# Order of the table work inside a look-up slot: low part and first count behind the look-ups, second count ahead of its pieces, table last

## The chip, the cores and the metric

The kernel runs on one core of a Trainium2 chip. The metric is the device time of one execution in microseconds. Before the change the median of three runs is 6,190.36 us (6,180.27 to 7,300.34).

## The reference, cut to what matters

Four graph layers over 16 graphs of 1,024 nodes with 128 features, each followed by a residual and a layer norm. The part that the change touches computes layer 1, the others run beside it or after it.

```python
# layer 0: masked attention over adj
# layer 1: for every node the maximum over its neighbours
p = jnp.einsum('bnd,do->bno', x, W1 - W2)
q = jnp.einsum('bnd,do->bno', x, W2)
pre = p[:, :, None, :] + q[:, None, :, :] + b
h = jax.nn.relu(pre) * adj[..., None]
out = jnp.max(h, axis=2)
# layer 2: sum over neighbours and a two-layer perceptron
# layer 3: a row-by-row thinning ("dilation") of adj that depends on the
#          rows before, then three graph convolutions with batch norms
```

## The kernel before, in words

The maximum over neighbours is done by tables. The 1,024 possible neighbours of a graph are cut into groups of six; for each group a table holds the maximum of q over each of its 64 subsets, and a node needs the entry of the subset that its row of the adjacency selects. Two groups (12 neighbours) make one **slot** s; a graph has NP = 86 slots, 16 graphs have 1,376. The look-up is a matmul with a one-hot matrix: 64 rows for one group, 64 for the other. Everything else that layers 0 to 2 and the dilation need is cut into **pieces** that are spread among the slots.

The names in `slot(s, last)`, which writes the order of the four engines out by hand (a manual schedule; a queue runs in the order in which the code is met):

- `look_up(s, i, pg)` (L839 to L845): four matmuls for half i (512 nodes) of slot s, the high and the low part of the table times the one-hot `hot`, into `pg`, a tile of two PSUM banks (tag "wide", two buffers). Both halves are looked up at the start of a slot. The VectorE line L911 takes the maximum of `pg` into `best`, once for each half.
- `count(s, h)` (L807 to L815): for half h of slot s one matmul counts on how many of the six neighbours each node's row agrees with each subset (`pm`, L814), and ScalarE turns the count into the one-hot `hot` (L815). `hot` has three buffers; the count runs two slots ahead of its look-up.
- `table(s)` (L817 to L830), every second slot: two transposes on TensorE bring the subset table of two slots from nodes by subsets into `pt` (L826); ScalarE copies it, rounded, to `high` (L829).
- `low_part(s)` (L832 to L836), every second slot, one slot later: a matmul subtracts `high` from `pt` in place (L834), and ScalarE copies the remainder to `low` (L836).
- `pm` and `pt` are tiles of one tag, "subset", with two buffers of a bank each.
- `advance(engines)` (L786 to L805) issues pieces: each stream (scores, attend, rest, tables_of) yields the engine and the cost of its next piece, and a piece is issued when the engine has room in this half slot, when its delay since the piece before has passed and when one of two "shared" PSUM banks is free, all by a virtual time `now` that counts slots. It is called for TensorE first, then for ScalarE, VectorE and GpSimd. `dilate_on()` does the same for the dilation, which has due times in slots.

A slot is worked in two halves, h = 0 and 1. In each half the order is: (half 0: both look-ups), pieces of TensorE, pieces of the others, a dilation piece, (half 0 of odd slots: low part), count of slot s + 2 for this half, (half 1 of even slots: table), `best` for this half. A piece of TensorE that VectorE evacuates is mostly evacuated in the next half slot; one that ScalarE evacuates, in the same one.

Of the kernel before, what the change touches and what calls it, by code (L numbers as in the profile page):

```python
# [74 lines left out]
def tile_graph_layers(ctx: ExitStack, tc, a, out):  # L75
# [166 lines left out]
    def layers_012():  # L242
# [133 lines left out]
        def attend(b):  # L376
            for t in range(T):
                yield ask("PE", 0.01, after=("e", b, t))
                if t == 0:
                    y = w4.tile([P, T, D], F32, name="y0", tag="xT")  # L380
                e, total = exps.pop((b, t))
                eT = w4.tile([P, T, P], F32, name="eT")
                for h in range(2):
                    yield ask("PE", 0.44, take=True, same=(h == 0))
                    p = shared("pe")
                    for c in range(4):
                        nc.tensor.transpose(p[:, c * P:(c + 1) * P],
                                            e[:, (4 * h + c) * P:(4 * h + c + 1) * P], ident)
                    yield ask("A", 0.59, give=True, same=True)
                    nc.scalar.copy(eT[:, 4 * h:4 * h + 4, :].rearrange("p c i -> p (c i)"), p)  # L390
                happened["back", b, t] = now
                for h in range(4):
                    yield ask("PE", 0.45, take=(h == 0), same=(h > 0))
                    if h == 0:
                        pav = shared("pav")[:, :D]
                    for c in range(2 * h, 2 * h + 2):
                        nc.tensor.matmul(pav, eT[:, c, :], values[b][:, c, :], start=(c == 0), stop=(c == T - 1))  # L397
                yield ask("V", 0.4, give=True)
                share = small.tile([P, 1], F32, name="share")
                nc.vector.reciprocal(share, total)  # L400
                nc.vector.scalar_tensor_tensor(y[:, t, :], pav, share, X[b][:, t, :], op0=ALU.mult, op1=ALU.add)
            yield from norm(X[b], y)
            happened["X1", b] = now
# [66 lines left out]
        def tables_of(b):  # L470

            if b:
                yield ask("V", 0, urgent=True, after=("tables", b - 1))
            for g0 in range(0, NP, TG):
                n_g = 2 * min(TG, NP - g0)
                yield ask("V", 0.01, same=True, urgent=True, after=("q", b))
                made.append((b, g0))
                yield ask("V", 0.1, same=True, urgent=True, after=("used", *made[-3]) if len(made) > 2 else None)
                qg = qs[b].rearrange("o (g s) -> o g s", s=GS)
                subs[b, g0] = w2.tile([P, TG, P], F32, name="sub", bufs=2)  # L480
                sub = subs[b, g0].rearrange("o t (a s) -> o (t a) s", a=2)
                nc.vector.memset(sub[:, :n_g, 0:1], LOWEST)
                for k in range(GS):
                    n = 1 << k
                    yield ask("V", 0.06 + n * n_g / 960, same=(n < 8), urgent=True)
                    nc.vector.tensor_max(sub[:, :n_g, n:2 * n], sub[:, :n_g, 0:n],  # L486
                                         qg[:, 2 * g0:2 * g0 + n_g, k:k + 1].to_broadcast([P, n_g, n]))
                happened["sub", b, g0] = now
            happened["tables", b] = now
# [255 lines left out]
        def load_x(b):  # L745
            X[b] = apool.tile([P, T, D], F32, name="X", bufs=3)
            nc.sync.dma_start(out=X[b], in_=x[b].rearrange("(t p) d -> p t d", p=P))
# [29 lines left out]
        def start(stream, first=False):  # L777
            pending[stream] = [next(stream, None), -9]
            streams.insert(0 if first else len(streams), stream)
# [27 lines left out]
        def count(s, h):  # L807

            b, g = divmod(s, NP)
            c, r = divmod(g, PC)  # L810
            if h == 0:
                hots[s] = w2.tile([P, N], F32R, name="hot", bufs=3)
            pm = psum.tile([P, 512], F32, tag="subset", name="pm", bufs=2)
            nc.tensor.matmul(pm, lit[:, r, :], AT[b * (T + 1) + c][:, halves[h]], start=True, stop=True)  # L814
            nc.scalar.activation(hots[s][:, halves[h]], pm, AF.Relu, bias=one_less)  # L815

        def table(s):  # L817

            b, g = divmod(s, NP)
            g0 = g - g % TG  # L820
            assert ("sub", b, g0) in happened, (s, [(x.__name__, pending[x]) for x in streams], room)
            pt = psum.tile([P, 512], F32, tag="subset", name="pt", bufs=2)[:, :2 * P]
            if g + 2 - g0 == min(TG, NP - g0):
                happened["used", b, g0] = now
            for k in range(2):
                nc.tensor.matmul(pt[:, k * P:(k + 1) * P], subs[b, g0][:, g - g0 + k, :], ident, is_transpose=True,  # L826
                                 start=(k == 0), stop=(k == 1))
            high = w2.tile([P, 2 * P], F32R, name="high", bufs=2)
            nc.scalar.copy(high, pt)  # L829
            tables[s] = pt, high  # L830

        def low_part(s):  # L832
            pt, high = tables[s]
            nc.tensor.matmul(pt, less, high, start=False, stop=True, skip_group_check=True)  # L834
            low = w2.tile([P, 2 * P], F32R, name="low", bufs=2)
            nc.scalar.copy(low, pt)  # L836
            tables[s] = high, low

        def look_up(s, h, pg):  # L839

            at = s % 2
            for k, part in enumerate(tables[s - at]):
                for a in range(2):
                    rows = slice(64 * a, 64 * a + 64)
                    nc.tensor.matmul(pg[:, a], part[rows, at * P:(at + 1) * P], hots[s][rows, halves[h]],  # L845
                                     start=(k == 0), stop=(k == 1))
# [16 lines left out]
        def slot(s, last):  # L863

            nonlocal now
            now = s
            b, g = divmod(s, NP)
            if s >= 0 and g == 0:
                bests[b] = bests[b - 1] if b else w4.tile([P, 2, N], F32, name="best")
                if b + 1 < B:  # L870
                    start(tables_of(b + 1), True)
                    load_x(b + 1)
                    start(attend(b + 1))
                    start(scores(b + 1))
            if s >= 0 and g % PC == 0:
                load_columns(b * (T + 1) + g // PC + 2)
            for h in range(2):
                now = s + 0.5 * h
                for e in ROOM:
                    room[e] = min(room[e] + ROOM[e] / 2, ROOM[e] / (2 if e in ("PE", "V") else 1))  # L880
                if s >= 0 and h == 0:
                    pgs = [psum.tile([P, 2, 512], F32, tag="wide", name="pg", bufs=2) for _ in range(2)]
                    for i in range(2):
                        look_up(s, i, pgs[i])
                early = s >= 0 and due < now
                if early:
                    dilate_on()
                advance(("PE",))
                advance(("A", "V", "Pool"))
                if s >= 0 and not early:  # L890
                    dilate_on()
                if h == 0 and s % 2 and s + 1 < last:
                    low_part(s + 1)
                if s + 2 < last:
                    count(s + 2, h)
                    if h and s % 2 == 0:
                        table(s + 2)
                if s >= 0:
                    own, pg = bests[b][:, :, halves[h]], pgs[h]
                    if g == 0:  # L900
                        if b:
                            if h:
                                merge(b - 1, h)
                            total(b - 1, h)
                        nc.vector.tensor_copy(own, pg)
                        if b and h:
                            start(rest(b - 1))
                    else:
                        if g == NP - 1 and h:
                            merge(b, 0)  # L910
                        nc.vector.tensor_max(own, own, pg)  # L911
            if s >= 0:
                hots.pop(s)
# [19 lines left out]
        with tc.manual_schedule(engines={mybir.EngineType.PE, mybir.EngineType.Activation, mybir.EngineType.DVE,  # L933
                                         mybir.EngineType.Pool}):
            for s in range(-2, B * NP):
                slot(s, B * NP)
# [10 lines left out]
            last = rest(B - 1)  # L947
# [426 lines left out]
```

## Time and profile before

| what | us |
|---|---|
| median of the runs shown | 6,190.36 |
| profiled execution, its time | 6,205.61 |
| its span on the core | 6,203.9 |
| TensorE busy | 5,426.3 (87%) |
| VectorE busy | 4,853.2 (78%) |
| ScalarE busy | 3,935.6 (63%) |
| GpSimd busy | 3,619.0 (58%) |
| mean granted TensorE clock | 0.965 |

The largest groups of instructions, by line:

| line, engine | what | count | busy us | mean ns | idle before it, us |
|---|---|---|---|---|---|
| L911 VectorE | best<-best,pg | 2,720 | 3,240.7 | 1,214 | 494.4 |
| L815 ScalarE | hot<-pm | 2,752 | 1,856.6 | 690 | 602.4 |
| L845 TensorE | pg<-hot,high | 5,504 | 1,325.7 | 477 | 254.8 |
| L845 TensorE | pg<-hot,low | 5,504 | 1,119.3 | 401 | 0.0 |
| L814 TensorE | pm<-AT,lit | 2,752 | 1,043.0 | 394 | 91.0 |
| L826 TensorE | pt<-ident,sub | 1,376 | 295.6 | 297 | 219.3 |
| L834 TensorE | pt<-high,less | 688 | 281.7 | 409 | 13.3 |
| L836 ScalarE | low<-pt | 688 | 256.4 | 373 | 504.8 |
| L829 ScalarE | high<-pt | 688 | 256.4 | 373 | 1.3 |

"Idle before it" is the time that the engine stood still just before such an instruction; the profile also says which instruction on which engine ended the wait. Matmul ends are modelled by the profiler. In rows of the list of waits the three numbers are the total in us, how often, and the longest. Weight loads (PEld) have rows of their own. In the timeline a row is the start, the duration, the engine, the line, what is written from what, how many instructions are merged in it, and in brackets the idle time before it.

### The profile page before, as it was taken

The numbers are of one execution on the slowest core, as the hardware profiler recorded it, in microseconds if no ns is written. First come the engines' busy times: TensorE is split into PE (matmuls) and PEld (weight loads), VectorE is DVE, ScalarE is ACT, GpSimd is POOL, SyncE is SP. The second block draws the span as 40 slices with busy tenths as digits, with TensorE's granted clock in tenths as the row PEclk, the third lists the DMA queues.
The fourth block names the chain that finished last, engine by engine and source line by source line (L and its number), as shares of the span: only waits on it lengthen the run. The fifth ranks groups of instructions, "written<-read, shape, count | busy, mean of one in ns | idle before, by whom it ended". The sixth has DMA issues, their size and how long they took to land.

```text
span 6203.9 us, 93371 instructions
## 1 busy us (share of the span) xinstructions
PE 5426.3 (87%) x30132; PEld 3090.5 (50%) x30250; DVE 4853.2 (78%) x7484; ACT 3935.6 (63%) x7362; POOL 3619.0 (58%) x11879
## 2 busy tenths in 40 slices
PE   5888888889898988888889898889888878999998
PEld 4545454545454545454545454545454435555654
DVE  2888888888888888888888888888888875555455
ACT  3666666666676666676667666666666554344865
POOL 2676666676666766667676767676667651110114
PEclk8999999999999999999999999999999989999999
DMA  5121213131212221222121212121121014554645
GB/s 41 12 34 23 40 23 40 23 41 24 39 23 36 28 40 24 37 30 37 27 41 25 37 27 39 24 39 25 32 31 29 15 43 124 160 142 129 218 163 191
DMA packets 496976, 334.29 MB, mean 54 GB/s; under 512 B 303338, under 2 KB 448228, under 8 KB 492388
## 3 DMA queue, kind: packets, MB, share of 16 engines
q1 hardware_dynamic: 405504, 260.29, 14.3%
q0 software_dynamic: 89008, 67.42, 12.6%
q8 instruction: 238, 3.90, 0.3%
q14 instruction: 254, 2.08, 0.1%
q10 hardware_dynamic: 1972, 0.59, 0.1%
HBM read 362.38 MB, written 133.96 MB: 80 GB/s over the span
## 4 chain that ended last, share of the span: by engine, by line
PE 29%; DVE 12%; ACT 5%; issue 3%; POOL 2%; DMA 1%; SPq 0%; DVEq 0%; ACTq 0%; POOLq 0%
PE pg L845 6%; DVE best L911 6%; PE pagg L1074 5%; PE pm L814 2%; PE po L1104 2%; ACT hot L815 2%; PE pav L397 1%; PE po L1098 1%; PE pa L439 1%; DVE sub L486 1%; PE pt L826 1%; PE pdeg L1029 1%; DVE near L1017 1%; PE pp L300 1%; PE prank L599 1%
## 5 line engine op out<-in xcount | busy, mean ns | idle before, releaser
L911 DVE TENSOR_TENSOR best<-best,pg 128x1024 f32<-128x1024 f32 x2720 | 3240.7, 1214 | 494.4 <-PE pg L845 485.3
L815 ACT ACTIVATE hot<-pm,one_less 128x512 fp32r<-128x512 f32 x2752 | 1856.6, 690 | 602.4 <-PE pm L814 591.5
L845 PE MATMUL pg<-hot,high 64*128 64x512 f32 x5504 | 1325.7, 477 | 254.8 <-DVE best L911 224.0
L814 PE MATMUL pm<-AT,lit 120*128 120x512 fp8e4 x2752 | 1043.0, 394 | 91.0 <-ACT low L836 84.5
L845 PE MATMUL pg<-hot,low 64*128 64x512 f32 x5504 | 1119.3, 401 | 0.0
L845 PEld LDWEIGHTS pg<-hot,high 64*128 64x128 f32 x5504 | 530.0, 188 | 1094.1 <-DVE best L911 570.4
L669 POOL TENSOR_SCALAR sc<-low_counts,half_mask,rest 16x1 f32<-16x1 f32 x992 | 357.1, 360 | 400.9 <-DVE rest L655 299.6
L836 ACT CAST low<-pt 128x256 fp32r<-128x256 f32 x688 | 256.4, 373 | 504.8 <-PE pt L834 503.7
L845 PEld LDWEIGHTS pg<-hot,low 64*128 64x128 f32 x5504 | 540.8, 191 | 30.4
L826 PE MATMUL pt<-ident,sub 128*128 128x128 f32 x1376 | 295.6, 297 | 219.3 <-ACT hot L815 213.3
L674 POOL TENSOR_SCALAR sc<-sc 16x1 f32<-16x1 f32 x992 | 394.7, 398 | 105.1
L826 PEld LDWEIGHTS pt<-ident,sub 128*128 128x128 f32 x1376 | 154.9, 143 | 487.9 <-ACT hot L815 465.3
L671 POOL TENSOR_SCALAR sc<-sc 16x1 f32<-16x1 f32 x992 | 318.5, 321 | 107.7
L1119 POOL TENSOR_TENSOR length<-length,mhalf 128x8 f32<-128x8 f32 x48 | 78.9, 1643 | 490.5 <-DVE length L1118 490.5
L676 POOL TENSOR_SCALAR hit<-V,sc 16x31 bf16<-16x31 bf16 (+30 forms) x992 | 362.6, 365 | 0.0
L677 POOL TENSOR_SCALAR last_rank<-V,sc 16x31 f32<-16x31 bf16 (+30 forms) x992 | 343.8, 347 | 0.0
L814 PEld LDWEIGHTS <-lit 120*128 120x128 fp8e4 x2752 | 236.8, 100 | 189.6 <-issue 105.4
L486 DVE TENSOR_TENSOR sub<-sub,q 128x24 f32<-128x24 f32 (+11 forms) x768 | 304.9, 398 | 24.6 <-ACT q L304 10.4
L397 PE MATMUL pav<-v,eT 128*128 128x128 f32 x2048 | 293.1, 287 | 2.9 <-ACT eT L390 2.0
L834 PE MATMUL pt<-high,less 128*128 128x256 f32 x688 | 281.7, 409 | 13.3 <-ACT high L829 13.0
L670 POOL TENSOR_SCALAR sc<-sc 16x1 f32<-16x1 f32 x992 | 239.5, 241 | 86.5
L397 PEld LDWEIGHTS pav<-v,eT 128*128 128x128 f32 x2048 | 263.3, 197 | 47.1 <-issue 20.8
(270 smaller groups left out, 9831.9 us busy)
## 6 DMA issues: line engine op xcount, KB each, us to landing
removed<-gone SPq DMA_DIRECT2D x128, 256.0 KB
An<-in_adj_dram POOLq DMA_DIRECT2D x16, 1024.0 KB, 14.9
E<-in_adj_dram POOLq DMA_DIRECT2D x128, 128.0 KB, 6.3
gone_all<-removed POOLq DMA_DIRECT2D x64, 256.0 KB, 10.3
near<-adj SPq DMA_DIRECT2D x16, 1024.0 KB
kept<-near SPq DMA_DIRECT2D x16, 1024.0 KB
share<-share SPq DMA_DIRECT2D x32, 512.0 KB
hidden<-r SPq DMA_DIRECT2D x32, 512.0 KB
```

Of the source, the lines that this page charges most:

```text
L397: nc.tensor.matmul(pav, eT[:, c, :], values[b][:, c, :], start=(c == 0), stop=(c == T - 1))
L486: nc.vector.tensor_max(sub[:, :n_g, n:2 * n], sub[:, :n_g, 0:n], qg[:, 2 * g0:2 * g0 + n_g, k:k + 1].to_broadcast([P, n_g, n]))
L669: gp.tensor_scalar(half, mine, half_mask[:, m], rest[:, n:n + 1], op0=ALU.mult, op1=ALU.add)
L671: gp.tensor_scalar(sf, half, 5.5, sf, op0=ALU.is_gt, op1=ALU.mult)
L674: gp.tensor_scalar(to, at, sf, none, op0=ALU.subtract, op1=ALU.subtract)
L676: gp.tensor_scalar(hit[:, n, n + 1:], V[:, n, n + 1:], at, None, op0=ALU.is_equal)
L677: gp.tensor_scalar(last[:, n + 1:], V[:, n, n + 1:], to, None, op0=ALU.is_le)
L814: nc.tensor.matmul(pm, lit[:, r, :], AT[b * (T + 1) + c][:, halves[h]], start=True, stop=True)
L815: nc.scalar.activation(hots[s][:, halves[h]], pm, AF.Relu, bias=one_less)
L826: nc.tensor.matmul(pt[:, k * P:(k + 1) * P], subs[b, g0][:, g - g0 + k, :], ident, is_transpose=True, start=(k == 0), stop=(k == 1))
L845: nc.tensor.matmul(pg[:, a], part[rows, at * P:(at + 1) * P], hots[s][rows, halves[h]], start=(k == 0), stop=(k == 1))
L911: nc.vector.tensor_max(own, own, pg)
```

## The change

The low part and the counts move ahead of the pieces of their half slot; the table stays behind them. Each slot issues the same instructions as before. In half 0 the order becomes look-ups, (odd slots: low part), first count, pieces; in half 1 it becomes second count, pieces, (even slots: table). `best` stays last in each half.

```diff
                     for i in range(2):
                         look_up(s, i, pgs[i])
+                if h == 0 and s % 2 and s + 1 < last:
+                    low_part(s + 1)
+                if s + 2 < last:
+                    count(s + 2, h)
                 early = s >= 0 and due < now
                 if early:
                     dilate_on()
                 advance(("PE",))
                 advance(("A", "V", "Pool"))
                 if s >= 0 and not early:
                     dilate_on()
-                if h == 0 and s % 2 and s + 1 < last:
-                    low_part(s + 1)
-                if s + 2 < last:
-                    count(s + 2, h)
-                    if h and s % 2 == 0:
-                        table(s + 2)
+                if s + 2 < last and h and s % 2 == 0:
+                    table(s + 2)
                 if s >= 0:
                     own, pg = bests[b][:, :, halves[h]], pgs[h]
```

## The prediction

> **What bounds the kernel now.** The windows came first. From 150 to 5,100 us the 1,376 slots of the table loop run; the rest (the later layers) is not touched, so only these 4,950 us count, 3.6 us a slot. In a steady thousand of them:
>
> ```profile
> core 0: us, PE busy (x) PEld busy (x) DVE busy (x) ACT busy (x) POOL busy (x), PEclk, DMA share, GB/s
> 2000.00:3000.00 1000.00, 882.69 (x5126) 496.77 (x5154) 862.04 (x1286) 683.51 (x1324) 704.60 (x2372) 0.98 0.23 33
> ```
>
> TensorE and VectorE are both near nine tenths and neither is full: they stop for each other and for ScalarE. The list of waits of the stretch 1000:5000 names whom for:
>
> ```profile
> PEld pg L845 <- DVE best L911: 457.7, 659, 2.5
> DVE best L911 <- PE pg L845: 391.0, 446, 5.0
> PEld pt L826 <- ACT hot L815: 372.0, 445, 2.9
> PE pg L845 <- DVE best L911: 181.0, 322, 2.9
> PE pt L826 <- ACT hot L815: 166.6, 285, 2.4
> PE pm L814 <- ACT low L836: 66.8, 222, 1.4
> PEld pt L834 <- ACT high L829: 44.8, 88, 1.4
> DVE e L352 <- PE psc L349: 43.7, 62, 1.3
> DVE y L401 <- PE pav L397: 32.6, 63, 1.9
> ```
>
> Two of TensorE's three large waits are for ScalarE, not VectorE: `table` (L826) waits for `hot`, a `count` (L814) for `low`. The tiles pm and pt share two "subset" banks; over two slots they are taken in the order pm, pm, pt, pm, pm, so pt takes the bank of the first count of its slot, and the second count of the following slot takes pt's. The timeline of TensorE and of ScalarE shows one such stop:
>
> ```profile
> 2513.74 1.08 PE L300 MATMUL pp<-hT,w_L_gnn_W 128*128 128x256 f32 x4
> 2514.66 0.38 PE L814 MATMUL pm<-AT,lit 120*128 120x512 fp8e4 x1
> 2514.88 0.59 PE L300 MATMUL pp<-hT,w_L_gnn_W 128*128 128x256 f32 x2
> 2515.31 0.38 PE L814 MATMUL pm<-AT,lit 120*128 120x512 fp8e4 x1
> 2516.88 0.44 PE L826 MATMUL pt<-ident,sub 128*128 128x128 f32 x2 [1.18 <-ACT hot L815]
> 2517.24 0.49 PE L845 MATMUL pg<-hot,high 64*128 64x512 f32 x2
> ...
> 2514.53 1.14 ACT L337 ACTIVATE off<-An,ones 128x1024 bf16<-128x1024 fp8e4 x1
> 2515.57 0.68 ACT L306 ACTIVATE z<-pp,w_L_gnn_b 128x512 f32<-128x512 f32 x1
> 2516.14 1.26 ACT L815 ACTIVATE hot<-pm,one_less 128x512 fp32r<-128x512 f32 x2
> ...
> 2518.01 2.35 DVE L911 TENSOR_TENSOR best<-best,pg 128x1024 f32<-128x1024 f32 x2 [3.14 <-PE pg L845]
> ```
>
> The first count was made at 2514.66, but its `hot` stood behind two stream pieces on ScalarE until 2516.14; the transposes wait for it, the look-ups stand behind the transposes, and VectorE, behind those, was idle for 3.14 us. The chain of waits (recorded from 2,983 us on) agrees: to 5,097 us its pieces are 989 us of TensorE, 601 of VectorE, 237 of ScalarE, 95 of that `hot`.
>
> **What the Trainium skill says.** "TensorE: Matmul & The Clock Gate", section "Step-by-step: what each phase is for": matmuls stay in program order and only weight loads are pulled ahead; the stop above agrees, the ready look-ups did not pass the transposes. "Perfetto Trace Analysis", section "Matmuls": independent groups should rotate through PSUM banks so that evacuation overlaps the next group; here they rotate, but 166.6 us show a rotation too short where the evacuation is queued late. The same page, "Identifying the Most-Contended Engine": busy TensorE time is a poor measure, since matmuls are pipelined. Agreed: one count lasts 0.38 us, but two in a row 0.60 (L814 x2 at 2530.33), so a count's slot in the queue is 0.22 and a modelled end hides 0.16 us of a stop behind it.
>
> **The change part by part.** The instructions are the same: VectorE's and GpSimd's lists are identical in order, TensorE's and ScalarE's are permuted inside a slot, and SP's DMAs are the same with a few `hit_p` and `adj8` issues exchanged with a neighbour; SP's transfers carry no wait in the table above, so I price this at nothing, and at up to 10 us if a `hit_p` comes late for VectorE. Piece placement is by virtual time, which the change leaves alone. Per slot, TensorE goes from look-ups, pieces 1, (low part), count 1, pieces 2, count 2, (table) to look-ups, (low part), count 1, pieces 1, count 2, pieces 2, (table).
>
> Gains. I sorted the slots of 1000:5000 in the timeline by whether TensorE has pieces in each half.
> - Table. Of 171 us idle before L826, 60.0 lie in 87 slots with pieces only in half 1, 24.5 in 249 with pieces in both, 86 in 217 without pieces in half 1. The new order puts pieces 1 between count 1 and the table, and `hot` ahead of ScalarE's own pieces, so the first two kinds go: half of it. Over the kernel L826 waited 213.3 us: 105 us. Where half 1 is empty nothing changes.
> - Second count. Of 68 us idle before L814 in odd slots, 40 lie where half 1 has pieces; these will stand between low part and second count. 40/68 of 84.5 us: 49 us.
> - Hidden ends. The removed stops are 162 at tables and 118 at counts in 4,000 us, 347 in the loop; at 0.15 us each (0.16, rounded down): 52 us. As low as 0 if the modelled ends are real.
> Together 206 us of TensorE. Do they lie on the path? Tables with pieces only in half 1 end slots of 3.91 us, odd slots of the same kind take 3.44; VectorE's own work there, two `best` of 1.21 us and pieces, does not fill them. So I take all of it.
>
> Costs.
> - Pieces 1 come later by a count (0.38 us) and in odd slots by low part and count (0.75). VectorE evacuates them in half 2, ahead of the second `best`. In the trace 177 such evacuations in 4,000 us start 0.1 to 0.6 us after their matmuls; delayed by 0.38 and 0.75 they would wait 74.5 us, 92 in the loop. VectorE has gaps to take it back (391 us for the look-ups): I charge a third, 30 us; ends 0 and 92.
> - Low part right behind the look-ups: it needs `high`, the last thing on ScalarE the slot before. In odd slots without pieces 1 it waited 10.2 us in 213, 0.05 each; the 341 others lose their cover: 16 us, 20 in the loop; ends 5 and 60, for `off` or `Exp` (1.15 us) can stand ahead of `high`. Behind it now wait count 1 and pieces 1.
> - Piece 2 on an evacuation of piece 1 (`pav` on `eT`, 0.59 us on ScalarE): odd slots lose the low part as cover and the evacuation follows a `hot`. Some 60 cases by 0.2: 12 us; ends 0 and 30.
> - Second count ahead of pieces 2: these are evacuated 0.2 us later; VectorE reads most of them a look-up later (0.3 to 2.3 us of slack). Nothing; up to 15 us.
> Sum: 206 - 30 - 20 - 12 = 144 us off the profiled 6,205.6 (span 6,203.9). That execution lies 15 us above the median of 6,190 (the runs shown are 6,180, 6,190 and a stray of 7,300), and the saving is set against the median: 6,190 - 144 = 6,046; rounded to **6,050 us**, 2.3% faster.
>
> **Rivals.**
> *The wait moves to VectorE (about 6,140).* With TensorE ahead, look-ups meet `best` of the slot before: L845 waits already 224.0 us for L911. For it: 601 us of the chain are VectorE's. Against: the bare slots, where VectorE binds, are not the ones that gain. At half the gain and the same costs: 103 - 62 = 41 us; with the hidden ends lost as well some 15; 6,135 to 6,175.
> *Late evacuations (about 6,320, slower).* One mechanism: pieces 1 late, so VectorE's evacuation late, so the second `best` late, so the next slot's second look-up, and the shared bank handed back late to the next piece, which stands ahead of a count and the look-ups in the queue. Its place is half 2 of every slot with a `psc`, `pav`, `pa`, `ph` or `py` in half 1, 220 in the loop. For it: the evacuation begins only 0.2 us after its matmul on the mean, so almost no slack covers the delay of 0.57. If all of the 92 us comes through and each costs again 0.57 at its bank (125 us), with a third of the gains (69) and 40 for the rest: 92 + 125 - 69 - 20 = 128, about 6,320. It decides once a late evacuation costs over 206/220 = 0.9 us. Against: TensorE still has the other shared bank, and pieces come at most every second half slot.
> *The change doesn't do what it says.* It does: the queue of TensorE has the low part and a count behind the look-ups in every slot, and 107 of the 688 tables no longer carry a wait for ScalarE at all. What may fail is the sorting above: gone only in part, it is the first rival.
>
> **How the numbers follow.** What a measurement of this kernel tells from no change is 2%, 124 us: 6,066 and 6,314 are the bounds. Forecast, with gains on the path: 0.57, 5,960 to 6,070 (costs at their low ends and shorter chains behind each stop add up to 206 + some 25; at the high ends of two costs the gain is 60). First rival, the unsorted remainder of the third with it: 0.31. Slower rival: 0.12, of which 0.08 passes 6,314. Of the forecast's 0.57, 0.55 lies under 6,066. So faster 0.55, same 0.37, slower 0.08; about 0.08 is left below the range and 0.11 above it. Range 5,960 to 6,200.
>
> **What would show it.** Right: L826's idle for `hot` falls from 213 to about 110 us and L814's for `low` from 84 to about 35; `best` waits less for `pg` (485 to about 350); L834 waits more for `high` (55 to about 75 on weight loads); L352 and L401 wait longer for their matmuls (84 and 70 together to some 240). Wrong, first rival: the same falls, but L845 waits for L911 by as much more. Wrong, second: `e`, `y` waits above 300 us and shared-bank waits at L348, L387, L300. A loop with unchanged L826 waits would mean that `hot` was late for another reason than its place behind the pieces.

## The result, and the profile after

The changed kernel takes 6,396.91 us (median of four runs, 6,389.82 to 6,400.03) against 6,189.4: **1.0339 of before, 95% interval 1.0318 to 1.0359**, 207 us slower. 6,050 was forecast. One run of the kernel before took 7,300 us, in the slow state, and is left out of the ratio.

The page of the changed kernel, its groups of instructions (busy us, mean ns | idle before, and who ended most of it):

```profile
L911 DVE TENSOR_TENSOR best<-best,pg 128x1024 f32<-128x1024 f32 x2720 | 3233.7, 1213 | 566.9 <-PE pg L845 561.1
L845 PE MATMUL pg<-hot,high 64*128 64x512 f32 x5504 | 1347.8, 485 | 407.7 <-DVE best L911 347.9
L814 PE MATMUL pm<-AT,lit 120*128 120x512 fp8e4 x2752 | 1058.5, 401 | 58.0 <-ACT low L836 55.9
L826 PE MATMUL pt<-ident,sub 128*128 128x128 f32 x1376 | 285.4, 290 | 107.8 <-ACT hot L815 104.2
L834 PE MATMUL pt<-high,less 128*128 128x256 f32 x688 | 275.0, 400 | 54.9 <-ACT high L829 53.4
```

The waits that the prediction counted on did shrink (the figures of before stand in the table ahead of the prediction): L826 stands idle 107.8 us where it was 219.3, L814 58.0 where it was 91.0. But the look-ups L845 wait 348 us for the maxima where it was 224, and the maxima wait longer for the look-ups too (561 us, before 485). Both engines that bind the loop stand still more for each other. The list of waits of the stretch 1000:5000 names what stands between them (total us, times, longest):

```profile
PE pg L845 <- DVE best L911: 259.8, 378, 2.7
PEld pt L834 <- ACT high L829: 115.6, 176, 2.2
DVE e L352 <- PE psc L349: 90.0, 92, 2.0
PE pt L826 <- ACT hot L815: 78.5, 139, 1.4
PE pe L387 <- ACT e L359: 55.4, 40, 2.3
DVE y L401 <- PE pav L397: 51.5, 73, 2.2
```

VectorE's waits for a piece to evacuate, L352 and L401, were 43.7 and 32.6 in the same stretch before, and L387's wait for the exponential 6.7. The timeline of TensorE and then of VectorE, in an odd slot, shows where they lead:

```profile
3197.76 0.50 PE L845 MATMUL pg<-hot,high 64*128 64x512 f32 x2 [0.28 <-DVE best L911]
3198.09 0.40 PE L845 MATMUL pg<-hot,low 64*128 64x512 f32 x2
3198.42 0.39 PE L834 MATMUL pt<-high,less 128*128 128x256 f32 x1
3198.66 0.39 PE L814 MATMUL pm<-AT,lit 120*128 120x512 fp8e4 x1
3198.88 0.39 PE L590 MATMUL pturn<-ident_b,E 128*128 128x128 bf16 x4
3199.11 0.38 PE L348 MATMUL psc<-off,penalty 128*128 128x512 bf16 x1
3199.32 1.03 PE L349 MATMUL psc<-kT,qT 128*128 128x256 f32 x4
...
3202.28 0.50 PE L845 MATMUL pg<-hot,high 64*128 64x512 f32 x2 [0.82 <-DVE best L911]
...
3200.39 0.69 DVE L352 TENSOR_SCALAR_CACHE_REDUCE e<-psc 128x512 f32<-128x512 f32 x1 [0.61 <-PE psc L349]
3201.00 0.08 DVE L352 DVE_READ_ACCUMULATOR e<-psc 128x1 f32 x1
3201.00 1.22 DVE L911 TENSOR_TENSOR best<-best,pg 128x1024 f32<-128x1024 f32 x1
```

This is a closed ring: second look-up (3197.76), low part and count, then the score pieces, done at 3200.35; VectorE has waited 0.61 us for them; evacuation; the second maximum; and only then the next slot's second look-up, 4.52 us after the first. Low part and count put 0.46 us (3198.42 to 3198.88) into this ring.

The loss lies in the loop. To see what it is made of I took, from the timelines, the time from the start of each matmul to the start of the next, less the tenth percentile for the same line and shape in the kernel before, over slots 200 to 1,300 ("stall"; idle time as printed misses what modelled ends hide). A slot went from 3,620 to 3,768 ns; times 1,376 slots that is 204 of the 207 us.

| stall ahead of, ns a slot | before | after |
|---|---|---|
| look-ups L845 | 375 | 537 |
| transposes of `e`, L387 | 42 | 88 |
| table L826 | 224 | 135 |
| low part L834, counts L814, other pieces | 55 + 277 + 237 | 157 + 283 + 136 |

The last row is nearly a swap (569 and 576). Single rows are rough: they add up to 126 of the 148 ns, and with other groupings of the same matmuls the look-ups' rise comes out between 120 and 210 ns, the last row's between -50 and +110.

The mean granted clock fell from 0.965 to 0.954, and this is a part of the loss. Between 1,000 and 5,000 us TensorE ran at half clock for 238 us before and 322 us after. Slots wholly at full clock went from 3,507 to 3,602 ns there, all slots from 3,612 to 3,764. The low clock follows stops: in the 3.4 us ahead of a half-clock stretch TensorE was busy 0.54 of the time before and 0.51 after, against 0.88 and 0.86 over the loop. So stops come ahead of the low clock, and the low clock adds to them. An upper estimate of what it added directly is half of the extra half-clock time, 44 of the 152 ns a slot. Much of the loss sits in few slots: the 1,165 that were at full clock in both kernels lose 50 ns each, the 104 that fell below it in the changed kernel alone lose 1.4 us each, stop and clock together.

### The profile page after: what moved, and what is told of

Read it like the earlier page. It is cut to its first block, busy times and chain, and to the rows that moved or that the text cites. A ratio compares the mean times of both kernels' runs of the same rounds, so it can differ in the third digit from the quotient of the medians.

```text
span 6396.8 us, 93315 instructions
## 1 busy us (share of the span) xinstructions
PE 5482.1 (86%) x30109; PEld 3171.4 (50%) x30250; DVE 4851.0 (76%) x7484; ACT 3951.1 (62%) x7362; POOL 3636.3 (57%) x11879
## 5 line engine op out<-in xcount | busy, mean ns | idle before, releaser
L845 PE MATMUL pg<-hot,high 64*128 64x512 f32 x5504 | 1347.8, 485 | 407.7 <-DVE best L911 347.9
L845 PE MATMUL pg<-hot,low 64*128 64x512 f32 x5504 | 1134.7, 406 | 0.0
L814 PE MATMUL pm<-AT,lit 120*128 120x512 fp8e4 x2752 | 1058.5, 401 | 58.0 <-ACT low L836 55.9
L845 PEld LDWEIGHTS pg<-hot,high 64*128 64x128 f32 x5504 | 538.3, 190 | 1139.9 <-DVE best L911 567.3
L845 PEld LDWEIGHTS pg<-hot,low 64*128 64x128 f32 x5504 | 550.9, 195 | 30.3
L674 POOL TENSOR_SCALAR sc<-sc 16x1 f32<-16x1 f32 x992 | 395.8, 399 | 104.8
L814 PEld LDWEIGHTS <-lit 120*128 120x128 fp8e4 x2752 | 228.5, 99 | 315.1 <-issue 259.7
L671 POOL TENSOR_SCALAR sc<-sc 16x1 f32<-16x1 f32 x992 | 319.1, 322 | 107.5
L826 PE MATMUL pt<-ident,sub 128*128 128x128 f32 x1376 | 285.4, 290 | 107.8 <-ACT hot L815 104.2
L834 PE MATMUL pt<-high,less 128*128 128x256 f32 x688 | 275.0, 400 | 54.9 <-ACT high L829 53.4
L826 PEld LDWEIGHTS pt<-ident,sub 128*128 128x128 f32 x1376 | 170.9, 145 | 257.9 <-ACT hot L815 224.1
L834 PEld LDWEIGHTS pt<-high,less 128*128 128x128 f32 x688 | 133.0, 193 | 326.6 <-issue 177.4
```

The lines of the kernel that those rows point to most:

```text
L674: gp.tensor_scalar(to, at, sf, none, op0=ALU.subtract, op1=ALU.subtract)
```

## The experiments

The theories: **A**, TensorE's first-half pieces are late behind low part and first count, so VectorE evacuates them late, ahead of its second maximum, for which the next second look-up waits. **B**, ScalarE's own pieces are late behind `hot`. **C**, the low part has lost its cover and holds the queue while it waits for `high`. "Idle a slot" in the expectations is printed idle time in 1000:5000 over the number of slots there. Each ratio is to the kernel before, run on the same chip beside it (medians 6,193 to 6,198 us).

**1. One part of the change alone.** Second half only:

```diff
+                if s + 2 < last and h:
+                    count(s + 2, h)
                 early = s >= 0 and due < now
...
-                if s + 2 < last:
+                if s + 2 < last and not h:
                     count(s + 2, h)
-                    if h and s % 2 == 0:
-                        table(s + 2)
+                if s + 2 < last and h and s % 2 == 0:
+                    table(s + 2)
```

> Only the second count goes ahead of its half slot's pieces; low part and first count stay behind the first half's pieces as before. Theory A (the slowdown is the first half's TensorE pieces, late by low part and first count: VectorE evacuates them late ahead of its second maximum, and the next slot's second look-up waits for that): those pieces stand where they stood before, so 0.99 to 1.005 of before, at most a third of the 3.4% lost; TensorE idle before L845 stays near 190 ns a slot (before 187, changed kernel 293). Theory B (ScalarE: a one-hot conversion of 0.69 us now stands ahead of ScalarE's evacuations in both halves, and banks come back late): about half of the loss, 1.015 to 1.02. Theory C (low part without cover waits for the rounded table): 1.00.

Measured: 1.0222 (1.0207 to 1.0238). No theory had it: B comes nearest, but for another reason. Its list of waits shows a stop of its own:

```profile
PE pm L814 <- ACT low L836: 187.1, 522, 1.8
PE pt L826 <- ACT hot L815: 161.7, 270, 2.5
```

Without pieces between them the second count follows first count and low part directly, and its bank is the one that ScalarE is still copying to `low` (66.8 us before). In the changed kernel the low part comes earlier, and this stop isn't there (40.9).

First half only:

```diff
+                if h == 0 and s % 2 and s + 1 < last:
+                    low_part(s + 1)
+                if s + 2 < last and not h:
+                    count(s + 2, h)
                 early = s >= 0 and due < now
...
-                if h == 0 and s % 2 and s + 1 < last:
-                    low_part(s + 1)
-                if s + 2 < last:
+                if s + 2 < last and h:
                     count(s + 2, h)
```

> Only the first half moves: low part and first count ahead of its pieces; the second count stays behind the second half's pieces. Theory A: nearly all of the loss, 1.028 to 1.035, and TensorE idle before L845 near 290 ns a slot. Theory B: half, 1.015 to 1.02. Theory C: all of it, with L834 idle for the rounded table at 40 ns a slot or more.

Measured: 1.0343 (1.0326 to 1.0361). The first half's move alone costs as much as the whole change; with it made, the second count's costs nothing more.

Of the first half, the low part alone (`low_part` moved, both counts left):

> Only the low part moves ahead of the first half's pieces; both counts stay behind theirs. Theory A: the pieces are late in odd slots alone and by 0.37 us, of a mean delay of 0.57 a third: 1.007 to 1.013. Theory B: no one-hot conversion moves, 1.00. Theory C: all of the loss, 1.03.

Measured: 1.0165 (1.015 to 1.0181), above A's figure and half of C's. And the first count alone (`count` for half 0 moved, low part and second count left):

> Only the first count moves ahead of the first half's pieces; the low part stays behind them. Theory A: pieces late by 0.38 us in every slot, two thirds of the delay, less what the table's shorter wait gives: 1.010 to 1.022. Theory B: about half, 1.015 to 1.02. Theory C: below 1.00, since the low part keeps its cover and the table's wait goes.

Measured: 1.0263 (1.0247 to 1.028). Above all three: the first count, right behind the look-ups, also waits for `hot` of the slot before to hand its bank back, a stop of which the kernel before has 3.0 us in the same stretch:

```profile
PE pm L814 <- ACT hot L815: 109.5, 198, 1.5
```

The parts don't add up: 1.7 and 2.6% alone, 3.4% together.

**2. One engine's order alone.** TensorE as before, ScalarE with low and hot ahead of its pieces:

```diff
                 advance(("PE",))
+                if h == 0 and s % 2 and s + 1 < last:
+                    low_part(s + 1)
+                if s + 2 < last:
+                    count(s + 2, h)
                 advance(("A", "V", "Pool"))
...
-                if h == 0 and s % 2 and s + 1 < last:
-                    low_part(s + 1)
-                if s + 2 < last:
-                    count(s + 2, h)
-                    if h and s % 2 == 0:
-                        table(s + 2)
+                if s + 2 < last and h and s % 2 == 0:
+                    table(s + 2)
```

> TensorE keeps the order of before (pieces, low part, count), but low part and count are issued ahead of ScalarE's pieces of the half slot, so that low and hot stand ahead of them on ScalarE alone. Theory A (TensorE's pieces are late behind low part and count): they are not late here, so no loss; the table's wait for hot falls as in the changed kernel, 0.98 to 1.00. Theory B (ScalarE's evacuations are late behind hot): the whole loss or more, 1.025 to 1.04, with banks and exponentials late, above all L387 waiting for L359.

Measured: 1.0424 (1.0405 to 1.0442), just above B's range. Here the look-ups' stall is as before (392 ns a slot), and the loss is in pieces that wait for ScalarE, above all

```profile
PE pe L387 <- ACT e L359: 85.8, 58, 2.1
```

(6.7 us before). The other corner splits `count` and `low_part` into their matmul, issued where the changed kernel has it, and their ScalarE line, where the kernel before has it:

```diff
+                if h == 0 and s % 2 and s + 1 < last:
+                    low_part(s + 1)
+                if s + 2 < last:
+                    pm = count(s + 2, h)
                 early = s >= 0 and due < now
...
-                    low_part(s + 1)
+                    low_copy(s + 1)
                 if s + 2 < last:
-                    count(s + 2, h)
+                    light(s + 2, h, pm)
```

> TensorE's order of the changed kernel with ScalarE's order of the kernel before: low part and first count (and the second count) ahead of the pieces on TensorE, their conversions low and hot behind ScalarE's pieces as before. With between (TensorE before, ScalarE changed, 1.042), the changed kernel (both, 1.034) and before (1.000) it fills the square. Theory A (late TensorE pieces, late evacuation by VectorE, late second maximum): the loss of the changed kernel stays, and the table's wait is back to 154 ns a slot: 1.03 to 1.05, L845 idle near 290 ns a slot. Theory B (ScalarE's evacuations behind hot): the loss goes, 1.00 to 1.01.

Measured: 1.0479 (1.0463 to 1.0495), inside A's range, but in part for a reason that A doesn't name. TensorE's idle time before the look-ups is 256 ns a slot, not the 290 of the changed kernel (188 before), and the second count waits for `low`, which now stands behind ScalarE's pieces (line numbers of that kernel; 40.9 us in the changed kernel):

```profile
PE pm L814 <- ACT low L842: 199.7, 332, 2.2
```

So either order alone costs more than both (1.034): in each of the two runs one queue waits for an item that the other has further back. Neither order alone explains the changed kernel, and the square doesn't show the shares of A and B.

**3. VectorE's second maximum set free.** All of VectorE's pieces behind the maximum of their half slot, in the changed kernel and in the one before:

```diff
-                advance(("A", "V", "Pool"))
+                advance(("A", "Pool"))
...
                         nc.vector.tensor_max(own, own, pg)
+                advance(("V",))
```

> The changed kernel, with VectorE's pieces issued behind the maximum of their half slot instead of ahead of it, so that the second maximum no longer stands behind a late evacuation. Theory A1 (the second maximum is late): most of the loss goes, 0.99 to 1.01, and VectorE's idle time before its evacuations (changed kernel 85 ns a slot before L352, 51 before L401) falls to a third. Theory A2 (what is late is the streams' own chain, score to VectorE to exponential to TensorE): worse than the changed kernel, 1.04 to 1.08, with L387 waiting over 100 ns a slot for L359.

> The kernel before with the same move of VectorE's pieces behind the maximum: the control of the run above. A1: little changes, 0.99 to 1.01, for VectorE waits for evacuated matmuls only some 100 ns a slot here. A2: slower, 1.01 to 1.04. The difference between this run and after_v_last is the loss that is left when the second maximum is free of evacuations.

Measured: 1.0189 (1.0172 to 1.0207) and 1.0075 (1.0059 to 1.0092). The first is between A1 and A2, the second inside A1. VectorE's idle time before `e` falls from 87 to 8 ns a slot, and of the 3.4% between the two orders 1.1 is left (1.0189 / 1.0075). The control shows that the move costs something itself; why wasn't tested, a likely reason is that it also puts pieces behind the first maximum, where VectorE has time for them. So the same for the second half alone:

```diff
-                advance(("A", "V", "Pool"))
+                advance(("A", "Pool") if h else ("A", "V", "Pool"))
...
                         nc.vector.tensor_max(own, own, pg)
+                if h:
+                    advance(("V",))
```

> The changed kernel with VectorE's pieces of the second half alone behind the second maximum (those of the first half stay ahead of the first). Only the second maximum is set free of the evacuation of the first half's late TensorE pieces. Theory A1 (the late evacuation holds the second maximum, and that the next slot's second look-up): the wait of the look-ups falls from 537 to about 420 ns a slot and two thirds of the loss go, 1.005 to 1.018. Theory A2 (the chain score, evacuation, exponential is what is late): no gain, 1.03 or more.

> The kernel before with the same edit, the control, and a candidate: in before the evacuations ahead of the second maximum wait some 110 ns a slot. A1: 0.99 to 1.00, the look-ups' wait of 375 ns a slot falls a little. A2: slower, 1.005 to 1.02, as with all of VectorE's pieces behind the maxima (1.0075).

Measured: **1.0007** (1.0 to 1.0015) and **0.9865** (0.9845 to 0.9885). Both are better than A1 expected. The first edit takes the whole 3.4% off the changed kernel, the second makes the fastest kernel of the study, 6,110.87 us. The list of waits of the first:

```profile
PE pg L845 <- DVE best L911: 166.5, 340, 2.2
PE pt L826 <- ACT hot L815: 84.5, 151, 1.4
PEld pt L834 <- ACT high L829: 158.1, 248, 2.2
PE pe L387 <- ACT e L359: 53.8, 39, 2.5
```

The look-ups' wait has gone back from 259.8 to 166.5 us, their stall from 537 to 381 ns a slot, and VectorE's idle time before `e` from 87 to 17; the table, low part and exponential wait as in the changed kernel. The order on TensorE, ScalarE and GpSimd is the same, instruction by instruction, with and without the edit, and the mean granted clock hardly differs (0.958 and 0.954), so the second maximum behind late evacuations was what cost most: with it free, the change costs 1.0007 / 0.9865 = 1.014, against 1.034.

**4. The 1.4% that are left.** Low part alone, first count alone, as in 1, with the second maximum free as in 3:

> before_v2_last (0.9865) with the low part alone moved behind the look-ups. If the rest of the loss is the low part's wait for the rounded table, with TensorE's queue behind it: 0.997 to 1.001 of before, i.e. most of the 1.4%. If it is the first count or the pieces' lateness: 0.987 to 0.992.

> before_v2_last (0.9865) with the first count alone moved behind the look-ups. If the rest is the low part's: 0.985 to 0.990 or better, since the table waits less. If it is the pieces, late by the count: 0.993 to 1.000. Without the free second maximum the same edit cost 2.6%; theory A1 expects it to cost under half of that here.

Measured: 0.9978 (0.9968 to 0.9988), which is 1.011 of `before_v2_last`, and 1.0021 (1.0003 to 1.0039), 1.016 of it. Each alone costs about what both cost. The low part is inside the range named for it, the first count just above the one for late pieces and above half of its 2.6%; a first count alone has the bank wait of experiment 1 besides. Since the two don't add up, the split of the last 1.4% stays open. The clock shows a difference between them, though. Against `before_v2_last`, a slot of `low_v2` is 48 ns longer, and 36 (standard error 8) where both are at full clock; a slot of `count1_v2` is 79 ns longer, but none (-16, standard error 13) where both are at full clock. So what the low part costs is mostly there at full clock, and what the first count costs lies in slots whose clock fell in one of the two traces (mean granted clock 0.949, against 0.968).

**5. The opposite of the change, and the table in another place.** The first half's pieces ahead of the second look-up:

```diff
-                    for i in range(2):
-                        look_up(s, i, pgs[i])
+                    look_up(s, 0, pgs[0])
...
                 advance(("PE",))
+                if s >= 0 and h == 0:
+                    look_up(s, 1, pgs[1])
```

> The kernel before with the first half's TensorE pieces between the two look-ups of a slot: these pieces are made earlier by one look-up (about 0.5 us), the second look-up comes later, when its bank is free. Theory A: the opposite of the change, so a gain: 0.97 to 0.99, the second look-up's wait for the second maximum (251 ns a slot before) and the waits of L352 and L401 fall. Theory B: ScalarE's order is unchanged, 1.00. Against: VectorE would wait for the second look-up where the pieces are long, 1.01.

Measured: 1.0027 (1.0018 to 1.0035). The miss is instructive: L845's wait for the maxima (L912 in that kernel) is smaller (111.2 us in 1000:5000, before 181.0), but theirs for L845 larger (442.9, before 391.0): most of what one engine no longer waits, the other does. With the second maximum free:

> before_v2_last with the first half's TensorE pieces between the two look-ups of a slot. With the second maximum free of evacuations the second look-up is needed at once behind the first maximum, so a later second look-up costs: A1 expects 0.99 to 1.005, worse than 0.9865; if the pieces' earliness is worth more than that, 0.97 to 0.985.

Measured: 1.0041 (1.0027 to 1.0055), inside the expectation of A. The table's transposes ahead of the second half's pieces and its low part behind the second count:

```diff
+                if s + 2 < last and h and s % 2 == 0:
+                    table(s + 2)
                 early = s >= 0 and due < now
...
-                if h == 0 and s % 2 and s + 1 < last:
-                    low_part(s + 1)
                 if s + 2 < last:
                     count(s + 2, h)
                     if h and s % 2 == 0:
-                        table(s + 2)
+                        low_part(s + 2)
```

> A kernel of the order before, with only the table's two parts moved: the transposes ahead of the second half's pieces in even slots, the low part behind the second count at the end of the same slot (it was one slot later). No piece of the first half moves on any engine. The two banks then go count, table, count, count, count, and each wait for a bank has a piece or a look-up as cover. Expected from the profile of before: L826 (154 ns a slot) and L814 (65) lose most of their idle time, up to 0.2 us of 3.61 a slot; 0.965 to 0.985. If the loss of the changed kernel were due to the table's or low part's place and not to the pieces', this would be slower than before. Against: pieces of the second half come 0.3 us later in even slots, 1.00.

Measured: 1.0031 (1.0018 to 1.0043): a miss. Two lines of its list of waits say why:

```profile
PE pm L814 <- ACT hot L815: 164.3, 292, 2.4
PE pg L845 <- DVE best L911: 269.8, 452, 3.5
```

The wait for `hot` has left L826 (3 ns idle a slot) and gone to the second count, which now takes the bank that the table took. The look-ups' wait for the maxima grew as well (181.0 before). With the same two banks and the same `hot`, the wait went to the next tile in the rotation.

## Why the prediction was wrong, step by step

- *Table* (105 us): right as a wait. L826's idle time fell by 111.5 us; as stall 89 ns a slot, 122 us.
- *Second count* (49 us): the idle time before L814 fell by 33 us. Together with low part and pieces its stall rose by 7 ns a slot, 10 us, so by that table nothing of it arrived.
- *Hidden ends* (52 us): not seen apart. The gains were to be 206 us; what can be seen is 122.
- **"Do they lie on the path? ... So I take all of it"** failed. In split_lookups and table_mid too, a stop taken from TensorE came back as a stop elsewhere. TensorE reaching the look-ups sooner gains nothing while the second maximum holds their bank.
- **"VectorE has gaps to take it back (391 us for the look-ups): I charge a third"** is the step that turned the sign. The gross lateness was sized well: L352 and L401 wait 230 us over the whole kernel (154 before; some 240 forecast), and VectorE's idle time before `e`, `y` and `gone` rose by 79 ns a slot, 109 us, where 92 were worked out. But it counted in full and was then passed on: the stall of the look-ups rose by 162 ns a slot, 223 us. VectorE's gaps lie ahead of the first maximum: of the 392 us that the maxima wait for the look-ups in 1000:5000 of the kernel before, all but 0.2 us stand there. The lateness falls ahead of the second (idle time before `e` there: 42 us before, 75 after), and that one releases the next slot's second look-up, which waits 275 us for it where it waited 190.
- *Low part on `high`* (20 us): waits of L834 for `high` rose from 55 to 149 us as weight loads and from 13 to 53 as matmuls. Under-priced; how much of it reaches the end was not settled.
- *Pieces on an evacuation of pieces 1* (12 us): `pav` was named, but it was the transposes of `e` that lost, behind the exponential: 46 ns a slot, 63 us. The exponential stands behind the late score and behind `hot`.
- *Second count ahead of pieces 2* at nothing: right by first_only and the changed kernel, 1.0343 and 1.0339, though alone it costs 2.2%.
- *The clock* isn't in the prediction. By the estimate above, the extra time at half clock cost at most 44 ns a slot directly, 61 us.
- *The rival in which the wait moves to VectorE* (6,140): its sign came true without its time. L826 and L814 wait 138 us less for ScalarE, L845 124 us more for the maxima. The sign doesn't tell a TensorE that arrives early from a maximum that comes late; experiment 3 does.
- *The rival of late evacuations* (6,320) named the ring that experiment 3 confirms, from pieces 1 to the second look-up. Its other half, the shared bank handed back late (125 us of its sum), isn't seen: L300, L348 and L349 do not wait notably longer. Nor did the waits of `e` and `y` pass the 300 us that were to be its sign. Its sum has a slip, too: 40 us are named for the rest, but 20 are taken off; with 40 added as costs it is 188 us, about 6,380. So its direction and ring were right, and its nearness to 6,397 is in part luck. The threshold of 0.9 us for each late evacuation set the gains at 206 us; with the 122 that came, it is 0.55, and the look-ups' 223 us alone are 1.0 for each of the 220. That it was given 0.12 was the same mistake as the third charged above.

## What to carry to other kernels

Before moving work ahead of other work in an in-order queue, follow what is pushed back through the next engine to the buffer that it frees: if the ring closes on the queue you started from, the delay can be paid in every turn, however much idle time the engines between show elsewhere. Look for the idle time at the place of the delay, not in the sum. And where the queues of two engines are written by hand, the cheapest cure may lie on the third: the second half's evacuations put behind the instruction that frees a bank gained 1.35% over the kernel before; with those of the first half moved too it lost 0.75%.

## What the runs showed of the hardware

After the 64-row look-ups, the first weight load of anything else began some 0.37 us after the last weight load of the look-ups, mostly with nothing to wait for ("issue" in the lists of waits): once a slot, median 0.365 us in both kernels, and hardly ever less than 0.36. The gap goes with the place and not with the instruction; 1000:5000, the kernel before and the changed one:

```profile
PEld L814 <- issue: 82.1, 219, 0.7
PEld pt L834 <- issue: 43.8, 114, 0.7
```

```profile
PEld L814 <- issue: 200.3, 524, 0.7
PEld pt L834 <- issue: 137.3, 355, 0.7
```

Low part and counts are met by it more often because they now follow the look-ups; 0.38 us a time in all four rows. In total these gaps are the same, 341 us before and 337 after. That fits the swap in the last row of the table of stalls, where the pieces lost about what these two gained; it wasn't tested apart. Why the gap is there no run shows.

Stretches at half clock, with short matmuls of 128 columns starting every 0.213 us in place of 0.112, came after 3.4 us in which TensorE was busy 0.54 of the time (kernel before, 49 stretches between 500 and 5,000 us) and 0.51 (changed, 70). No run varied the stops and nothing else, so what brings such a stretch about stays open.
